# Norms whose last step ScalarE takes, with one root for a double norm, router norms by pairs, and layer 1's attentions as two lanes

## The chip, the cores and the metric

The kernel runs on one core of a Trainium2 chip. A core has engines that each work through their own instruction stream in order: TensorE (PE in the profile; its weight loads are listed as PEld), VectorE (DVE), ScalarE (ACT), GpSimd (POOL) and SyncE (SP, which only issues transfers here). They wait for each other by semaphores. Data lies in SBUF (128 partitions); TensorE's results lie in PSUM. The metric is the device time of one execution in microseconds (us); the number for a kernel is the median over runs. One further execution is profiled, and the trace tells when every instruction began and ended.

## The reference

A transformer of four layers, 4 sequences of 512 tokens, width 128, all in float32. Each layer is a "macaron": half a feed-forward part, attention, half the same feed-forward part again, each behind a layer norm without parameters.

```python
def _layernorm(x, axis=-1, eps=1e-05):
    return (x - mean(x)) / sqrt(var(x) + eps)

x = x + 0.5 * ffn_l(_layernorm(x))
x = x + attn_l(_layernorm(x))
x = x + 0.5 * ffn_l(_layernorm(x))       # l = 0, 1, 2, 3
```

The feed-forward part of layer 0 is a mixture of experts with two experts for a token, that of layer 2 one in which each expert picks its tokens, that of layer 3 one with one expert for a token. Layer 1's is dense, with ternary weights:

```python
h = silu(tlin(x, w1, s1)) * tlin(x, w2, s2)      # 128 -> 512
h = gelu(tlin(h, h1, hs1))                       # 512 -> 512
h = gelu(tlin(h, h2, hs2))                       # 512 -> 512
return tlin(h, w3, s3)                           # 512 -> 128
```

Layer 1's attention holds a layer norm of its own, with gamma and beta, so two norms follow one another there:

```python
h = _layer_norm(hidden_states, gamma, beta)
keys = h @ Wk.T + bk ; values = h @ Wv.T + bv
w = exp((keys @ Wka.T + bka) / sqrt(128))
w = w / cumsum(w, axis=1)
return cumsum(w * keys, axis=1) * values
```

The result has to be right to float32's precision, since the routers compare logits; matmuls in layer 1 split their data into three bfloat16 parts for that reason.

## The kernel before

x stays in SBUF from beginning to end as 128 partitions by 4 sequences (b) by 4 tiles of tokens (t) by 128. The program is written in one Python function. Each engine's instructions are put in order by a scheduler, which goes by what is ready and by the order in which the program issues them; the engine then keeps that order strictly, so an instruction placed too early makes all that stands behind it wait.

**Norms.** `layer_norm` (L247) does one sequence: on VectorE four `bn_stats` (L255) and four `bn_aggr` (L257) give mean and variance `mv`; `inverse_root` (L223) makes 1/sqrt(var + eps) by integer bit arithmetic and three Newton steps, 13 small instructions on 128x4 values, each needing the one before; then four `tensor_scalar` (L267), (x − mean) · root, give `xn`. With `twice` (layer 1's attention) the variance of the once normalised values is worked out (L262, L263), a second root is taken, and the two are multiplied (L265). `transposed` (L301) turns a norm on TensorE, tile `ps`, and copies it by ScalarE into xT.

**Layer 1** (`l1`, L1000 and on). The sequences go by pairs, (0, 1) and (2, 3). For each b of a pair come `first` (four groups o of six matmuls into `p`, silu on ScalarE into `sl`, the product ha_a on VectorE, L1035), and then for both b `hidden` with the first 512x512 matrix (name b) and `hidden` with the second (name c), in each four groups o of 12 matmuls with a gelu behind (L1052). `leave` (L1058 and on) multiplies by w3 (48 short matmuls into `po`) and adds to x on VectorE (L1067, L1068). `take_apart` (L990 and on) makes, after every group, the middle part `hr` on VectorE (L992) and the low part `hl` (L993), on GpSimd where o is even, on VectorE where it is odd.

The four attentions between the two feed-forward parts are generators. `pieces` is a list of such generators, and `step(pieces)` at the end of every group o runs the first of them on to its next `yield`, the next one only when that is done. So an attention's norm, its transposes (`ps_a`, after one yield), hT (L1092), the keys pk, the logits pka, the values pv, the scan cs (L1104), the reciprocal rc (L1106), two GpSimd products kw (L1107, L1108), the second scan and the product o (L1112, L1113), and the transposes back `po_a` are strewn into the matrix groups. In the same list stand the `begin`s (L1010) of the pair that comes next: norm g, transposes `ps_g`, copy, three parts. Attentions of b = 0, 1 lie in the groups of the first part's pair (2, 3); those of b = 2, 3 in the groups of the second part's pair (0, 1).

**Routers.** `l2_ffn` (loop at L1179) and `l3_ffn` (loop at L1449) go over the four b: norm (c in layer 2, d in layer 3), transposes, copy xT, four small matmuls into `lg`; `lb` (L1193 in layer 2) adds the bias to all 16 tiles of logits, and the routing begins. The loops also send x or xn to DRAM from SP. Each runs twice (0 and 1 in the names).

**Attentions of layers 2 and 3** call `layer_norm` once for each b (a2, L1384; a3, L1664). In layer 2, o_wk (L1393) and mn_k (L1375) are VectorE's steps on keys behind the projections. Layer 0 has norms of its own, in pieces, which do not use this function.

## Time and profile before

| | us |
|---|---|
| median of 3 runs (lowest, highest) | 1663.09 (1662.7, 1671.05) |
| the profiled execution | 1666.47 |
| its span, first to last instruction | 1664.7 |
| layer 0 (feed-forward, attention, feed-forward) | 0 to 562 |
| layer 1 | 562 to 855 |
| layer 2: feed-forward, attention, feed-forward | 855 to 975, to 1017, to 1135 |
| layer 3: feed-forward, attention, feed-forward | 1135 to 1271, to 1527, to 1665 |

The mean clock that TensorE was granted over the span is 0.886 of the full one. Names in the profile have their buffer numbers cut off: `xn_a` is any xn of an attention's norm, `ps_a` its transposes; of names that end in the letter of a `hidden` or `first`, `ha_a`, `hr_a` and `hl_a` are the three parts after `first`, those with b and c after the two `hidden`. A row names line, engine, operation and out<-in.

### The profile page before, as it was taken

The numbers are of one execution on the slowest core, as the hardware profiler recorded it, in microseconds if no ns is written. First come the engines' busy times: TensorE is split into PE (matmuls) and PEld (weight loads), VectorE is DVE, ScalarE is ACT, GpSimd is POOL, SyncE is SP. The second block draws the span as 40 slices with busy tenths as digits, with TensorE's granted clock in tenths as the row PEclk, the third lists the DMA queues.
The fourth block names the chain that finished last, engine by engine and source line by source line (L and its number), as shares of the span: only waits on it lengthen the run. The fifth ranks groups of instructions, "written<-read, shape, count | busy, mean of one in ns | idle before, by whom it ended". The sixth has DMA issues, their size and how long they took to land.

```text
span 1664.7 us, 24721 instructions
## 1 busy us (share of the span) xinstructions
PE 1355.9 (81%) x8372; PEld 849.3 (51%) x8372; DVE 1025.0 (62%) x3179; ACT 668.1 (40%) x1413; POOL 582.6 (35%) x811
## 2 busy tenths in 40 slices
PE   3999899999899987979983646363885899998685
PEld 2898533443698633434552534252784233334685
DVE  4547787787446678888757267625214788883311
ACT  1433477777423323333320212020342377775242
POOL 0354265450255252222210730171784110100585
PEclk9999899999899998989985867585897699998698
DMA  8022212120311010004021221023643422311445
GB/s 322 26 67 59 47 51 64 45 54 17 123 61 49 22 52 1 1 1 190 14 64 30 40 60 53 11 37 82 213 150 100 95 60 57 66 33 28 121 167 183
DMA packets 97144, 121.26 MB, mean 73 GB/s; under 512 B 12223, under 2 KB 85428, under 8 KB 95481
## 3 DMA queue, kind: packets, MB, share of 16 engines
q1 hardware_dynamic: 76393, 69.84, 14.8%
q0 software_dynamic: 15968, 44.98, 9.1%
q10 hardware_dynamic: 4656, 4.86, 0.9%
q8 instruction: 66, 1.08, 0.3%
q14 instruction: 61, 0.50, 0.1%
HBM read 91.88 MB, written 27.79 MB: 72 GB/s over the span
## 4 chain that ended last, share of the span: by engine, by line
PE 64%; DVE 14%; DMA 7%; POOL 6%; issue 5%; SPq 2%; ACT 2%; POOLq 0%; DVEq 0%; ACTq 0%
PE pa L162 9%; PE po L162 7%; PE av L162 7%; PE smax L162 6%; PE sexp L162 6%; PE pc L162 6%; PE pb L162 4%; PE p3b L162 3%; PE lg L162 2%; PE p3a L162 2%; DMA sum<-y,idx 2%; PE p L162 2%; POOL y L1608 2%; PE pq L162 1%; DVE mp L718 1%
## 5 line engine op out<-in xcount | busy, mean ns | idle before, releaser
L718 DVE TENSOR_REDUCE mp<-smax 128x1 f32<-128x512 f32 (+1 forms) x512 | 326.7, 684 | 57.3 <-PE smax L162 56.4
L756 ACT ACTIVATE e<-sexp 128x512 f32<-128x512 f32 x512 | 271.3, 599 | 99.5 <-PE sexp L162 98.4
L162 PE MATMUL smax<-keys,queries 72*128 72x512 bf16 x512 | 200.6, 403 | 11.4 <-DMA queries<-rows_q 4.6
L162 PE MATMUL sexp<-queries,keys 75*128 75x512 bf16 (+1 forms) x512 | 193.1, 388 | 6.2 <-DMA queries<-mT 4.5
L162 PEld LDWEIGHTS <-th 128*128 128x128 bf16 x768 | 74.0, 96 | 97.4 <-issue 4.8
L543 ACT ACTIVATE gl<-pa 128x256 f32<-128x256 f32 x160 | 61.3, 383 | 154.8 <-PE pa L162 115.0
L162 PEld LDWEIGHTS <-queries 72*128 72x128 bf16 x512 | 51.9, 102 | 134.3 <-issue 82.3
L1557 POOL DMA_INDIRECT xg<-xd,src x46 | 46.8, 1018 | 175.3 <-DVE wi L1547 168.1
L544 DVE TENSOR_TENSOR hid<-pa,gl 128x256 f32<-128x256 f32 x160 | 67.3, 422 | 58.7 <-ACT gl L543 58.4
L162 PE MATMUL po<-we,hid 128*128 128x128 f32 x768 | 91.7, 276 | 0.0
L162 PEld LDWEIGHTS po<-we,hid 128*128 128x128 f32 x768 | 90.7, 192 | 1.9
L610 POOL DMA_INDIRECT yg<-y,idx x64 | 66.6, 1040 | 52.5 <-DMA y<-y 42.1
L162 PE MATMUL pa<-ei,we 128*128 128x256 f32 (+1 forms) x352 | 82.7, 390 | 1.5 <-DVE x L910 0.8
L162 PE MATMUL pa<-xTe,we 128*128 128x256 f32 (+1 forms) x352 | 81.8, 381 | 1.0 <-DVE xTe L532 1.0
L162 PEld LDWEIGHTS <-keys 75*128 75x128 bf16 (+1 forms) x512 | 50.2, 100 | 57.7 <-issue 15.5
L162 PEld LDWEIGHTS pa<-ei,we 128*128 128x128 f32 (+1 forms) x352 | 67.1, 196 | 11.5 <-ACT ei L644 1.5
L361 POOL MEMSET paced<- 128x256 f32 x218 | 71.7, 329 | 0.3
L162 PE MATMUL av<-e,v 128*32 128x512 f32 x512 | 70.7, 623 | 0.0
L162 PEld LDWEIGHTS pa<-xTe,we 128*128 128x128 f32 (+1 forms) x352 | 64.6, 189 | 11.8 <-issue 1.4
L162 PE MATMUL av<-e,vp 128*32 128x512 f32 x512 | 68.7, 604 | 0.0
L496 POOL DMA_INDIRECT slots<-xn,idx x32 | 31.4, 982 | 87.7 <-DVE idx L214 82.7
L1308 POOL DMA_INDIRECT xg<-xd,idx x32 | 31.3, 977 | 86.5 <-DVE junk L1289 78.3
(446 smaller groups left out, 2934.8 us busy)
## 6 DMA issues: line engine op xcount, KB each, us to landing
we<-in_w0p_dram SPq DMA_DIRECT2D x8, 1080.0 KB
we<-in_e_pack_dram SPq DMA_DIRECT2D x8, 963.0 KB
queries<-rows SPq DMA_DIRECT2D x48, 96.0 KB
queries<-rows_q SPq DMA_DIRECT2D x48, 96.0 KB
y<-y SPq DMA_DIRECT2D x32, 128.0 KB
xd<-xn_c SPq DMA_DIRECT2D x8, 272.0 KB
slots<-zero ACTq DMA_DIRECT2D x2, 1024.0 KB
xs<-slots SPq DMA_DIRECT2D x16, 128.0 KB
```

The source lines that it names most:

```text
L162: return turn_of(nc.tensor.matmul(*a, **k))
L361: zeros = nc.gpsimd.memset(paced, 0.0)
L496: m = nc.gpsimd.indirect_dma_start(out=slots_of[half][:, :], out_offset=rows_in(idx[:, i, t : t + 1]), in_=xn[:, t, :], in_offset=None, bo ...
L543: nc.scalar.activation(gl, pa[:, 0], AF.Gelu_apprx_tanh)
L544: latest["ins"] = nc.vector.tensor_tensor(hids[e][:, c, :], pa[:, 1], gl, op=ALU.mult)
L610: m = nc.gpsimd.indirect_dma_start(out=yg[:, t, i], out_offset=None, in_=y_d[:, :], in_offset=rows_in(idx[:, i, t : t + 1]), bounds_check= ...
L718: return nc.vector.tensor_reduce(out=self.mp[i][:, t, j], in_=s, axis=AX.X, op=ALU.max, negate=True)
L756: return e, nc.scalar.activation(e, s, AF.Exp, scale=scale)
L1308: m = nc.gpsimd.indirect_dma_start(out=t, out_offset=None, in_=xd[:, :], in_offset=rows_at(e, h))
L1557: m = nc.gpsimd.indirect_dma_start(out=xg[i], out_offset=None, in_=xd[:, :], in_offset=rows_at(src, i), bounds_check=T - 1, oob_is_err=False,)
L1608: m = nc.gpsimd.indirect_dma_start(out=y_d[:, :], out_offset=rows_at(to, i), in_=y, in_offset=None, bounds_check=T - 1, oob_is_err=False,)
```

## The change

The norm's last step becomes an activation of ScalarE, Identity of rs · x + nb, with rs and nb = −mean · rs as one number for each partition; nb is one more VectorE instruction. `layer_norms` takes several sequences together and makes one root for all of them; `layer_norm` is that with one. The double norm takes one root: with var for the first norm's variance, its double root is 1/sqrt((1 + eps) · var + eps²), so only the first line of `inverse_root` differs. 144 xn instructions go from VectorE to ScalarE: 16 each of both begins g, the attentions a of layers 1, 2 and 3, and the routers c and d of both executions.

The routers go over pairs of b: one root of eight columns for a pair, both pairs of transposes, both copies, then the logits of both. xT has three buffers there, and xn in layer 3 three.

In layer 1 `pieces` keeps the begins, and the attentions stand in two lists, `attending[0]` and `attending[1]`, by b; `go_on` at each group o steps all three. Between an attention's norm and its transposes lie five yields in place of one, and one yield less in front of the second scan. `begin` has one yield more and first runs the attentions to their end. `hidden` leaves the low part to GpSimd for every o, except in the first part's pair (0, 1): 24 of the 128x512 low parts change from VectorE to GpSimd.

In the instruction streams VectorE has 2837 instructions after for 3145 before, ScalarE 1568 for 1426 (29 table loads for 31), GpSimd 840 for 816; TensorE and SP have as many as before, and SP's order is the same. In TensorE's order the transposes ps_a of b = 0 and b = 2 stood in front of the last group of `first` of the pair's first sequence, and now stand in the third group of `first` of its second sequence; those of b = 1 and b = 3 stood in the third group of that `first`, and now stand in the third group of the `hidden` that follows.

```diff
@@ -220,7 +220,7 @@
 
     behind = Behind()
 
-    def inverse_root(var, n, name, bufs=4, vector=None, eng=None):
+    def inverse_root(var, n, name, bufs=4, vector=None, eng=None, twice=False):
 
 
         def tmp(tag, dt=F32):
@@ -229,7 +229,10 @@
         vector = vector or nc.vector
         v, h, t, y = (tmp(i) for i in ("v", "h", "t", "y"))
         i = tmp("i", I32)
-        vector.tensor_scalar(v, var, EPS, None, op0=ALU.add)
+        if twice:
+            vector.tensor_scalar(v, var, 1.0 + EPS, EPS * EPS, op0=ALU.mult, op1=ALU.add)
+        else:
+            vector.tensor_scalar(v, var, EPS, None, op0=ALU.add)
         vector.tensor_scalar(i, v.bitcast(I32), 1, None, op0=ALU.logical_shift_right)
         vector.tensor_scalar(y.bitcast(I32), i, -1.0, float(0x5F3759DF), op0=ALU.mult, op1=ALU.add)
         on = eng or vector
@@ -244,31 +247,33 @@
                 on.scalar_tensor_tensor(y, t, 1.5, y, op0=ALU.add, op1=ALU.mult)
         return y
 
-    def layer_norm(pool, src, name, bufs=2, width=D, twice=False):
-
-        if not isinstance(src, list):
-            src = [src[:, t, :] for t in range(TT)]
-        st = small.tile([P, TT, 6], F32, tag="ln_st", name=f"st_{name}")
-        mv = small.tile([P, TT, 2], F32, tag="ln_mv", name=f"mv_{name}")
-        xn = pool.tile([P, TT, width], F32, tag="xn", bufs=bufs, name=f"xn_{name}")
-        for t in range(TT):
-            nc.vector.bn_stats(out=st[:, t, :], in_=src[t])
-        for t in range(TT):
-            nc.vector.bn_aggr(out=mv[:, t, :], in_=st[:, t, :])
-        rs = inverse_root(mv[:, :, 1], TT, name)
-        if twice:
-
-            v2 = small.tile([P, TT], F32, tag="ln_v2", name=f"v2_{name}")
-            nc.vector.tensor_tensor(v2, rs, rs, op=ALU.mult)
-            nc.vector.tensor_tensor(v2, v2, mv[:, :, 1], op=ALU.mult)
-            r2 = inverse_root(v2, TT, f"2{name}")
-            nc.vector.tensor_tensor(rs, rs, r2, op=ALU.mult)
-        for t in range(TT):
-            nc.vector.tensor_scalar(
-                xn[:, t, :D], src[t], mv[:, t, 0:1], rs[:, t : t + 1],
-                op0=ALU.subtract, op1=ALU.mult,
-            )
-        return xn
+    def layer_norms(pool, srcs, name, bufs=2, width=D, twice=False):
+
+        n = len(srcs) * TT
+        st = small.tile([P, n, 6], F32, tag=f"ln_st{n}", name=f"st_{name}")
+        mv = small.tile([P, n, 2], F32, tag=f"ln_mv{n}", name=f"mv_{name}")
+        nb = small.tile([P, n], F32, tag=f"ln_nb{n}", name=f"nb_{name}")
+        for i in range(n):
+            nc.vector.bn_stats(out=st[:, i, :], in_=srcs[i // TT][:, i % TT, :])
+        for i in range(n):
+            nc.vector.bn_aggr(out=mv[:, i, :], in_=st[:, i, :])
+
+
+        rs = inverse_root(mv[:, :, 1], n, name, twice=twice)
+        nc.vector.scalar_tensor_tensor(nb, mv[:, :, 0], -1.0, rs, op0=ALU.mult, op1=ALU.mult)
+        out = []
+        for q, src in enumerate(srcs):
+            xn = pool.tile([P, TT, width], F32, tag="xn", bufs=bufs, name=f"xn_{name}_{q}")
+            for t in range(TT):
+                i = q * TT + t
+                nc.scalar.activation(
+                    xn[:, t, :D], src[:, t, :], AF.Identity, scale=rs[:, i : i + 1], bias=nb[:, i : i + 1]
+                )
+            out.append(xn)
+        return out
+
+    def layer_norm(pool, src, name, **options):
+        return layer_norms(pool, [src], name, **options)[0]
 
     def norm_in_pieces(pool, src, name, bufs=1, eng=None):
 
@@ -1002,14 +1007,31 @@
 
         s1, s2, hs1, hs2 = (take(pcl, PCOL, n) for n in ("s1", "s2", "hs1", "hs2"))
         xs, act = {}, {}
-        pieces = list(aside)
+        pieces, attending = list(aside), ([], [])
 
         with tc.tile_pool(name="l1f", bufs=1, reuse_waits="tile") as wk, \
              tc.tile_pool(name="l1a", bufs=2, reuse_waits="tile") as wa:
 
+            def go_on():
+
+                step(attending[0])
+                step(attending[1])
+                step(pieces)
+
+            def finish():
+                for r in pieces + attending[0] + attending[1]:
+                    run(r)
+                for r in (pieces, *attending):
+                    r.clear()
+
             def begin(k, b):
                 nm = f"{k}_{b}"
+                for a in attending:
+
+                    while a:
+                        step(a)
                 xn = layer_norm(wk, x[:, b], f"g{nm}")
+                yield
                 yield
                 ps = tr_bank([P, S], f"ps_g{nm}")
                 for t in range(TT):
@@ -1036,7 +1058,7 @@
                         act[b].all[:, o], p2[1], s2[:, o : o + 1], sl, op0=ALU.mult, op1=ALU.mult
                     )
                     latest["ins"] = act[b].take_apart(o, nc.gpsimd if o % 2 == 0 else None)
-                    step(pieces)
+                    go_on()
 
             def hidden(k, b, w, sc, name):
                 nm = f"{k}_{b}"
@@ -1050,8 +1072,9 @@
                                 start=(c == 0 and j == 0), stop=(c == 3 and j == 2),
                             )
                     nc.scalar.activation(act[b].all[:, o], pa, AF.Gelu, scale=sc[:, o : o + 1])
-                    latest["ins"] = act[b].take_apart(o, nc.gpsimd if o % 2 == 0 else None)
-                    step(pieces)
+                    low = o % 2 == 0 or k or b > 1
+                    latest["ins"] = act[b].take_apart(o, nc.gpsimd if low else None)
+                    go_on()
 
             def leave(k, b):
                 nm = f"{k}_{b}"
@@ -1084,7 +1107,8 @@
                     return ps
 
                 xn = layer_norm(wa, x[:, b], f"a1_{b}", twice=True)
-                yield
+                for _ in range(5):
+                    yield
                 ps = tr_bank([P, S], f"ps_a1_{b}")
                 for t in range(TT):
                     transpose(ps[:, t * P : (t + 1) * P], xn[:, t, :], ident)
@@ -1106,7 +1130,6 @@
                 nc.vector.reciprocal(rc, cs)
                 nc.gpsimd.tensor_tensor(kw, kw, kT, op=ALU.mult)
                 nc.gpsimd.tensor_tensor(kw, kw, rc, op=ALU.mult)
-                yield
                 yield
                 pooled, o = tmp("pooled", 1), tmp("o")
                 nc.vector.tensor_tensor_scan(pooled, one, kw, 0.0, op0=ALU.mult, op1=ALU.add)
@@ -1127,23 +1150,19 @@
                         if last:
                             leave(*last.pop(0))
                             if k + p[0] and not (k == 1 and p[0] == 2):
-                                pieces.append(attention((b + 2) % 4))
+                                attending[b % 2].append(attention((b + 2) % 4))
                         first(k, b)
                     for b in p:
                         hidden(k, b, th1, hs1, "b")
                     if (k, p[0]) == (0, 0):
-                        for r in pieces:
-                            run(r)
-                        pieces.clear()
+                        finish()
                         then()
                     nk, nb = (k, 2) if p[0] == 0 else (k + 1, 0)
                     if nk < 2:
                         pieces += [begin(nk, nb), begin(nk, nb + 1)]
                     for b in p:
                         hidden(k, b, th2, hs2, "c")
-                    for r in pieces:
-                        run(r)
-                    pieces.clear()
+                    finish()
                     last = [(k, b) for b in p]
             for r in last:
                 leave(*r)
@@ -1176,18 +1195,18 @@
             sums_of[k, 0] = dram.tile([T, D], F32, tag=f"s{k}0", name=f"sum_{k}_0")
             xns = []
             lg = acc_bank([P, NT, NE], f"lg2_{k}")
-            for b in range(B):
-                xn = layer_norm(wk, x[:, b], f"c{k}_{b}", bufs=B, width=W)
-                xns.append(xn)
-                xT = transposed(wk, xn[:, :, :D], f"c{k}_{b}")
-                for t in range(TT):
-                    matmul(
-                        lg[:, b * TT + t, :], lhsT=xT[:, t * P : (t + 1) * P], rhs=take(mat, MAT, "wr2"),
-                        start=True, stop=True,
+            for p in ((0, 1), (2, 3)):
+                xns += layer_norms(wk, [x[:, b] for b in p], f"c{k}_{p[0]}", bufs=B, width=W)
+                xTs = [transposed(wk, xns[b][:, :, :D], f"c{k}_{b}", bufs=3) for b in p]
+                for b, xT in zip(p, xTs):
+                    for t in range(TT):
+                        matmul(
+                            lg[:, b * TT + t, :], lhsT=xT[:, t * P : (t + 1) * P], rhs=take(mat, MAT, "wr2"),
+                            start=True, stop=True,
+                        )
+                    nc.sync.dma_start(
+                        out=sums_of[k, 0][b * S : (b + 1) * S, :].rearrange("(t p) d -> p t d", p=P), in_=x[:, b]
                     )
-                nc.sync.dma_start(
-                    out=sums_of[k, 0][b * S : (b + 1) * S, :].rearrange("(t p) d -> p t d", p=P), in_=x[:, b]
-                )
             lb = tmp([P, NT, NE], "lb")
             br = take(rws, ROW, "br2").unsqueeze(1).to_broadcast([P, NT, NE])
             nc.vector.tensor_tensor(lb, lg, br, op=ALU.add)
@@ -1446,16 +1465,16 @@
             xd = dram.tile([T, D], F32, tag=f"xd{k}", name=f"xd_{k}")
             y_d = dram.tile([T, D], F32, tag=f"y3{k}", name=f"y3_{k}")
             lg = acc_bank([P, NT, NE], f"lg3_{k}")
-            for b in range(B):
-                nm = f"{k}_{b}"
-                xn = layer_norm(wk, x[:, b], f"d{nm}")
-                nc.sync.dma_start(out=xd[b * S : (b + 1) * S, :].rearrange("(t p) d -> p t d", p=P), in_=xn)
-                xT = transposed(wk, xn, f"d{nm}")
-                for t in range(TT):
-                    matmul(
-                        lg[:, b * TT + t, :], lhsT=xT[:, t * P : (t + 1) * P], rhs=take(mat, MAT, "wr3"),
-                        start=True, stop=True,
-                    )
+            for p in ((0, 1), (2, 3)):
+                xns = layer_norms(wk, [x[:, b] for b in p], f"d{k}_{p[0]}", bufs=3)
+                for b, xn in zip(p, xns):
+                    nc.sync.dma_start(out=xd[b * S : (b + 1) * S, :].rearrange("(t p) d -> p t d", p=P), in_=xn)
+                for b, xT in [(b, transposed(wk, xn, f"d{k}_{b}", bufs=3)) for b, xn in zip(p, xns)]:
+                    for t in range(TT):
+                        matmul(
+                            lg[:, b * TT + t, :], lhsT=xT[:, t * P : (t + 1) * P], rhs=take(mat, MAT, "wr3"),
+                            start=True, stop=True,
+                        )
             lb = tmp([P, NT, NE], "lb")
             br = take(rws, ROW, "br3").unsqueeze(1).to_broadcast([P, NT, NE])
             nc.vector.tensor_tensor(lb, lg, br, op=ALU.add)
```

## The prediction

> **What bounds the kernel now.** I read the page's busy shares first, then the windows of the stages that the diff touches, then who TensorE waits for in layer 1, and last the timelines of one router and of the attentions' norms.
>
> ```profile
> PE 1355.9 (81%) x8372; PEld 849.3 (51%) x8372; DVE 1025.0 (62%) x3179; ACT 668.1 (40%) x1413; POOL 582.6 (35%) x811
> ```
>
> Over the whole span TensorE is the fullest engine and ScalarE (ACT) has room; the shares are averages, so the stages decide.
>
> ```profile
> core 0: us, PE busy (x) PEld busy (x) DVE busy (x) ACT busy (x) POOL busy (x), PEclk, DMA share, GB/s
> 562.00:855.00 293.00, 263.46 (x1432) 128.02 (x1431) 237.68 (x611) 100.80 (x136) 86.95 (x89) 0.95 0.11 38
> ...
> 640.00:690.00 50.00, 41.07 (x167) 17.98 (x168) 44.82 (x126) 21.28 (x27) 12.50 (x11) 0.90 0.00 0
> 690.00:720.00 30.00, 28.73 (x207) 16.13 (x205) 24.73 (x70) 9.00 (x13) 5.76 (x6) 1.00 0.01 1
> 720.00:770.00 50.00, 39.85 (x157) 17.41 (x158) 43.43 (x125) 20.59 (x26) 11.82 (x10) 0.90 0.17 66
> ...
> 982.00:1017.00 35.00, 28.42 (x160) 21.52 (x160) 32.20 (x140) 13.14 (x21) 6.12 (x5) 0.89 0.08 24
> ```
>
> Each row is a stretch: its length, each engine's busy time, the granted clock. Layer 1 lasts 293 us and TensorE works 263 of them. Where two attentions run (640 to 690, 720 to 770), VectorE (DVE) is busy 44.8 and 43.4 of 50 us and the clock falls to 0.90, against 1.00 between. Layer 2's attention (982 to 1017) is VectorE's: 32.2 of 35.
>
> ```profile
> engine line waited for: us in total, times, longest us
> PE ps_a L165 <- DVE xn_a L267: 16.0, 2, 8.0
> PE ps_g L165 <- DVE xn_g L267: 6.4, 2, 5.5
> PE p L162 <- DVE ha_a L1035: 2.5, 2, 1.3
> ```
>
> These are TensorE's waits in layer 1 alone. Two of 8.0 us, one for each pair of attentions, are for the norm in front of the attention (637.9 and 718.7 us): its transposes were placed on TensorE before VectorE had got through the double root. The 5.5 us wait is for a norm whose x comes late from layer 0's gathers.
>
> ```profile
> 1022.45 1.11 DVE L267 TENSOR_SCALAR xn_c<-x,mv_c,ir_y_c 128x128 f32<-128x128 f32 x4
> ...
> 1024.45 1.12 DVE L267 TENSOR_SCALAR xn_c<-x,mv_c,ir_y_c 128x128 f32<-128x128 f32 x4
> ```
>
> ```profile
> 1021.56 1.88 PE L162 MATMUL lg<-mat,xT_c 128*128 128x8 f32 x8 [0.73 <-ACT xT_c L301]
> 1025.12 1.88 PE L162 MATMUL lg<-mat,xT_c 128*128 128x8 f32 x8 [0.73 <-ACT xT_c L301]
> 1028.67 1.88 PE L162 MATMUL lg<-mat,xT_c 128*128 128x8 f32 x8 [0.73 <-ACT xT_c L301]
> ```
>
> A router's end: VectorE has its last norm at 1025.6, TensorE works until 1030.5. A period of 3.55 us per b is transposes 1.09, copy of xT 0.58, lg 1.88, one after another; 0.73 of it TensorE waits for the copy.
>
> **What the new operations cost.**
>
> ```profile
> L1092 ACT ACTIVATE hT<-ps_a,pcl x4: 777/777/779, 647.1 to 739.4; 128x512 f32<-128x512 f32 x4
> ```
>
> ```profile
> L1587 ACT ACTIVATE h3a<-p3a,wd x120: 358/368/378, 1202.5 to 1647.3; 128x128 f32<-128x128 f32 x120
> ```
>
> No 128x128 Identity with scale and bias per partition stands in the trace. hT is that form at 512 columns: 0.78 us (min/median/max in ns). ScalarE's copy of that size takes 0.58, so a pointer costs about 0.10. h3a, 128x128 with one pointer, takes 0.37; one pointer more gives an estimate of 0.46 us for an xn, the value I take, as it is nearest. Bounds: 0.37 and 0.78. In a row they overlap; four h3a take 1.14 us, so with 0.09 more each I put four xn at 1.5 us and eight at 2.9. On VectorE four take 1.11.
>
> [...]
>
> **The change part by part.**
>
> VectorE loses 144 xn of 0.28 us (40 us), 24 low parts of 0.69 (16.5), and 168 short root instructions (four attentions times 16, four routers times 26), and gains 28 nb: some 75 us of 1025. ScalarE gains 144 xn, 50 to 66 us on 668. GpSimd gains 24 low parts of 1.04 (25 us). Nothing ahead of layer 1 moves.
>
> *Layer 1's start* (wait of 0.9 us at 562.5): the norm's last steps leave VectorE: 0.3 won, 0 to 0.9. The 5.5 us wait stays, since its x is late: 0.
>
> *The attentions.* In TensorE's new order the first norm's transposes of a pair stand nearly four groups of `first` later (each six matmuls of 0.222 us, 1.33), 5.3 us of work; the second norm's stand in the third group of the next `hidden`. The double root is 14 instructions shorter, which follow each other at 0.20 us: 2.8. Together 8.1, so the 8.0 us wait goes, with the 0.9 us wait for hT behind it, and the clock: 41.07 us of TensorE work at 0.90 would take about 37 at 1.00, 4.5 with the second stall's part. 13.4 us per pair are to be had. What is late next: a group of `first` needs ha 0.74, hr 0.68 and half of hl's 0.69 on VectorE, 1.8 us, against 1.33 on TensorE; with the wait no longer between, five groups in a row put TensorE 5 × 0.45 = 2.2 us ahead of ha. hT stays at 0.9. The second norm's nb stands on VectorE behind the first lane's scan (1.22), reciprocal (3.35) and second scan; its xn then go through ScalarE: 2.5. pk behind it: 1.3. Together 6.9, and I take off 1.5 for a clock that these stalls hold down. 13.4 − 6.9 − 1.5 = 5.0 per pair, two pairs 10.0. Bounds per pair: −2 (every new stall doubled) and 8. VectorE's relief of 16 xn and the roots is in these stalls already.
>
> [...]
>
> *Low parts on GpSimd.* A group of `hidden` is 12 matmuls of 0.222, 2.67 us; 1.04 on GpSimd fits, and the other b of the pair lies between maker and user. The last one is ready about 0.5 us before its use. Cost 0; without that cover 0.35 us at each of three hand-overs. What it frees on VectorE is not waited for there, so nothing is won either.
>
> *Routers by pairs.* From the last x to lb is now 13.3 us (856.9 to 870.3), 13.3 and 14.3. New: stats 0.9, aggregates 0.4, root 14 × 0.20, nb 0.2, 4.3 in all; eight xn 2.9, for both copies of xT are queued behind all eight on ScalarE; the first copy 0.6; two lg at 1.8, the second copy beside the first of them: 4.3 + 2.9 + 0.6 + 3.6 = 11.4. Won: 1.9 in each of layer 2's two, 2.9 in layer 3's second. What it costs: x of b=2 waits for the root of b=3. Layer 3's first starts from x that come one by one, so the pair's wait eats most: 0.9, between −1 and 2. Bounds for the four: 0 (xn at 0.78) and 10. The stores of x on SP keep their order and are not waited for by lg.
>
> *Layer 2's attention.* VectorE loses 16 xn, 4.4 us, in a stretch where it is full, and ScalarE (13.1 of 35) takes them between its own; o_wk and mn_k queue behind: 2.5, between 0 and 4. *Layer 3's attention:* the first xT, q and k copies now queue behind four xn on ScalarE: −0.8, between −2 and 0.
>
> Sum: 0.3 + 10.0 + 1.9 + 1.9 + 2.9 + 0.9 + 2.5 − 0.8 = 19.6 us. The profiled execution took 1666.5 us (span 1664.7), 3.4 above the median of the runs; from the median 1663.1 − 19.6 = 1643.5.
>
> **Rivals.**
>
> *A. The lanes only move the wait.* The 16 us of waits turn into the same sum at ha, o and the second norm. For it: VectorE is 90% busy there. Against: 75 us leave it. Layer 1 wins 0 to 2, the rest 9, less up to 5 where the same happens: 1653 (1651 to 1659).
>
> *B. All of it comes.* No new stall, 13.4 twice, routers and attention at their upper bounds: 27 + 9 + 4 = 40, of which I take off 8 for stages that go on into a wait for DMAs: about 1631. Against: the reciprocal and scans stay.
>
> *C. Slower: GpSimd and VectorE in each other's way.* In the trace a short root instruction that met a GpSimd low part took 1.02 us (639.2) in place of 0.16, a VectorE hl 1.65 in place of 0.69, the GpSimd one 1.5. All 24 new low parts fall in `hidden`, where lane 2's root stands between scans. If each holds VectorE 0.9 us on that chain (22 us) and ScalarE's xn wait for it with the gelu of the next group behind them, TensorE stalls in `hidden` as well. It decides once a group costs VectorE over 2.67 us; then the layer, in place of winning 10, loses 22, and the other 9 are won: 1663 + 22 − 9 = 1676. Against: hr alone is 0.68 of 2.67.
>
> [...]
>
> *D. It doesn't do what it says.* An xn on ScalarE takes 0.78 and the double root by pairs leaves x of b=2 and b=3 both late: routers 0, attentions 0, layer 1 half: about 1659.
>
> **How the numbers follow.** About 0.5% (8.3 us: below 1654.8, above 1671.4) is what a measurement here can tell from no change. Forecast 1644 (1637 to 1651): 0.50. A 0.20, half of it within 0.5%. B 0.12. C 0.10. D 0.08, within 0.5%. Faster 0.50 + 0.12 + 0.10 = 0.72; same 0.10 + 0.08 = 0.18; slower 0.10. The range is to take in B's near end, A and D: 1628 to 1664; C is left out.
>
> **What would show it.** TensorE's waits ps_a for xn at 2.5 us or less, not 8.0; layer 1 near 283 us; VectorE some 75 us less busy; xn on ScalarE at 0.46; lb about 11.4 us after the last x. Wrong if ps_a, po_a or ha waits sum to over 16 us in layer 1, if hl on GpSimd runs well over 1.04, or if layer 2's attention does not shrink.

## The result

Over 16 runs of each kernel, side by side, the changed one takes 1653.54 us (1647.96 to 1663.75) and the one before 1666.59 (1661.51 to 1675.62). The ratio is 0.9921 with a 95% interval of 0.9903 to 0.9939: 13.2 us faster, between 10.2 and 16.2. The forecast was 19.6 us. The time lies in the stated range (1628 to 1664), but above the likeliest case's own (1637 to 1651), at the figure of rival A (1653); 13.2 us off the 1663.1 that the forecast started from would be 1649.9. The profiled execution of the changed kernel took 1654.42 us (span 1652.6).

The page's busy shares of the changed kernel:

```profile
PE 1354.9 (82%) x8347; PEld 844.5 (51%) x8372; DVE 965.5 (58%) x2871; ACT 720.8 (44%) x1555; POOL 610.0 (37%) x835
```

VectorE lost 60 us of work (75 were forecast), ScalarE gained 53 and GpSimd 27, and the span lost 12: what VectorE was relieved of is mostly not what ended a stage. An xn takes 0.48 us, for 0.46 in the forecast (here those of the attentions; min/median/max in ns):

```profile
L269 ACT ACTIVATE xn_a<-x,nb_a,ir_y_a x48: 477/482/515, 639.0 to 1280.9; 128x128 f32<-128x128 f32 x48
```

TensorE's waits in layer 1, the same view as in the prediction:

```profile
PE ps_a L165 <- ACT xn_a L269: 9.6, 4, 3.6
PE ps_g L165 <- ACT xn_g L269: 5.5, 1, 5.5
PE pk L162 <- ACT hT L1116: 3.5, 4, 0.9
```

Two waits of 8.0 us have become four, 1.4 and 3.6 us in the first pair of attentions, 1.4 and 3.2 in the second. Behind the longer ones the granted clock is 0.50. TensorE's timeline at the first of them, and the windows of 2 us behind it (columns as in the prediction; the figure behind POOL's is the granted clock):

```profile
657.56 0.48 PE L165 MATMUL ps_a<-cst,xn_a 128*128 128x128 f32 x1 [3.62 <-ACT xn_a L269]
...
660.82 1.22 PE L162 MATMUL pk<-hT,mat 128*128 128x512 f32 x1 [0.87 <-ACT hT L1116]
```

```profile
657.50:659.50 2.00, 1.94 (x8) 1.69 (x9) 0.08 (x1) 1.73 (x5) 0.98 (x1) 0.50 0.00 0
659.50:661.50 2.00, 1.13 (x4) 0.56 (x3) 1.72 (x5) 0.78 (x1) 0.35 (x1) 0.50 0.00 0
661.50:663.50 2.00, 2.00 (x4) 0.45 (x3) 1.79 (x14) 0.56 (x1) 0.69 (x1) 0.50 0.00 0
663.50:665.50 2.00, 2.00 (x6) 0.74 (x5) 1.01 (x7) 0.61 (x2) 0.00 (x0) 0.50 0.00 0
665.50:667.50 2.00, 2.00 (x7) 0.82 (x6) 0.00 (x0) 0.00 (x0) 0.00 (x0) 0.62 0.00 0
667.50:669.50 2.00, 2.00 (x7) 0.79 (x6) 0.69 (x1) 1.85 (x3) 0.38 (x1) 1.00 0.00 0
```

Behind the wait, half clock lasts from 657.5 to about 667, 9.5 us, in which TensorE is busy 8.6: the 128x512 matmuls of `hidden` begin every 0.43 us there (663.55 to 666.53), for 0.22 at 1.00 (652.23 to 653.56). The clock is at half also behind the 1.4 us wait of the second pair, from 721.6 to 725.0; behind the same waits in the first pair (1.4 us for the first norm, 0.9 for hT) it stays at 1.00:

```profile
636.29:639.70 3.41, 2.01 (x10) 0.75 (x9) 3.41 (x11) 1.34 (x3) 0.00 (x0) 1.00 0.00 0
639.70:643.11 3.41, 2.45 (x9) 0.98 (x10) 3.41 (x15) 2.23 (x5) 1.04 (x1) 1.00 0.01 2
718.21:721.62 3.41, 1.62 (x7) 0.79 (x8) 3.41 (x15) 2.88 (x6) 1.04 (x1) 1.00 0.00 0
721.62:725.03 3.41, 3.41 (x7) 1.03 (x7) 3.41 (x9) 1.05 (x2) 1.40 (x1) 0.50 0.00 0
```

These windows are 3.41 us long for a reason. In the traces of both kernels all times between two changes of the clock, over the whole span, are whole multiples of 3.41 us. In the changed kernel's pairs the changes come at 656.77, 667.01, 721.62, 725.03, 738.69 and 745.51, which are 3, 16, 1, 4 and 2 times 3.41 us apart. In the 3.41 us in front of its three falls TensorE was busy 0.59, 1.62 and 0.43 us. In the first pair the grid parts the two short waits, TensorE is busy 2.01 and 2.45 us of the two stretches, and the clock stays at 1.00; in the second pair both waits fall into one, 1.62 us are busy, and the next stretch runs at half clock. So the same two waits went with either clock. The grid also lies elsewhere in each of the two executions: 641.30, a fall in the kernel before, and 656.77 here are 4.5 times 3.41 us apart.

Why the second norm is late stands in VectorE's timeline:

```profile
647.75 0.15 DVE L242 TENSOR_TENSOR ir_t_a<-ir_t_a,ir_h_a 128x4 f32<-128x4 f32 x1
647.82 1.22 DVE L1128 TENSOR_TENSOR_SCAN cs<-cst,kw 128x512 f32<-128x512 f32 x1
648.95 0.14 DVE L247 SCALAR_TENSOR_TENSOR ir_y_a<-ir_t_a,ir_y_a 128x4 f32<-128x4 f32 x1
649.07 3.35 DVE L1130 RECIPROCAL rc<-cs 128x512 f32<-128x512 f32 x1
652.34 0.10 DVE L241 TENSOR_TENSOR ir_t_a<-ir_y_a 128x4 f32<-128x4 f32 x1
...
652.95 1.24 DVE L242 TENSOR_TENSOR ir_t_a<-ir_t_a,ir_h_a 128x4 f32<-128x4 f32 x1
654.21 2.05 DVE L1135 TENSOR_TENSOR_SCAN pooled<-cst,kw 128x512 f32<-128x512 f32 x1
656.17 0.13 DVE L247 SCALAR_TENSOR_TENSOR ir_y_a<-ir_t_a,ir_y_a 128x4 f32<-128x4 f32 x1
...
656.83 0.15 DVE L263 SCALAR_TENSOR_TENSOR nb_a<-mv_a,ir_y_a 128x4 f32<-128x4 f32 x1
```

Between two steps of its root lies one long instruction of the other lane or of the ternary part. From 647.75 to the end of nb at 656.98, 9.2 us, the norm's own six short instructions (five of the root, and nb) take 1.9, and 1.24 of that is one that met a GpSimd product.

The stages of the two profiled executions, measured between the same instructions:

| stage | before | after | won | forecast |
|---|---|---|---|---|
| layer 1, first pair of attentions | 80.8 | 79.5 | 1.3 | 5.0 |
| layer 1, second pair | 82.0 | 79.4 | 2.6 | 5.0 |
| last x to lb, layer 2 (two routers) | 13.3, 14.1 | 11.2, 12.0 | 4.2 | 3.8 |
| the same, layer 3 (first, second) | 21.3, 39.9 | 19.8, 37.2 | 4.2 | 3.8 |
| layer 2's attention | 40.7 | 40.4 | 0.3 | 2.5 |
| layer 3's attention, to its first scores | 25.6 | 26.4 | −0.8 | −0.8 |

A pair runs from the first short matmul of the `leave` behind one pair of sequences to that behind the next, which is the same work in every kernel. Layer 2's second router and layer 3's two are counted from somewhat earlier events than in the prediction, the end of the attention's matmuls, the first statistics and the last scores; the differences are not touched by that. The sum is 11.8 us, and layer 1's start and rest add 0.6. What else differs between the two executions is not the change's: up to the first `hidden`, 577.1 us against 573.0, hardly anything is touched, and the twelve executions below have from 571.7 to 584.3 there; the expert stage of layer 2, 105.5 before and 108.4 after, has 105.5 to 108.9 in those twelve with the same code.

### The profile page after: what moved, and what is told of

Read it like the earlier page. It is cut to its first block, busy times and chain, and to the rows that moved or that the text cites. A ratio compares the mean times of both kernels' runs of the same rounds, so it can differ in the third digit from the quotient of the medians.

```text
span 1652.6 us, 24561 instructions
## 1 busy us (share of the span) xinstructions
PE 1354.9 (82%) x8347; PEld 844.5 (51%) x8372; DVE 965.5 (58%) x2871; ACT 720.8 (44%) x1555; POOL 610.0 (37%) x835
## 4 chain that ended last, share of the span: by engine, by line
PE 62%; DVE 14%; POOL 8%; DMA 7%; issue 5%; ACT 3%; SPq 2%; POOLq 0%; DVEq 0%; ACTq 0%
PE pa L162 9%; PE po L162 7%; PE av L162 7%; PE smax L162 7%; PE sexp L162 6%; PE pc L162 6%; PE p3b L162 3%; PE pb L162 3%; POOL y L1627 2%; DMA sum<-y,idx 2%; PE p L162 2%; PE p3a L162 2%; PE lg L162 2%; PE pq L162 1%; POOL paced L366 1%
## 5 line engine op out<-in xcount | busy, mean ns | idle before, releaser
L162 PEld LDWEIGHTS <-keys 75*128 75x128 bf16 (+1 forms) x512 | 50.2, 100 | 58.4 <-issue 14.1
L162 PEld LDWEIGHTS pa<-xTe,we 128*128 128x128 f32 (+1 forms) x352 | 64.7, 189 | 11.8 <-issue 1.4
```

What stands on the lines that cost most here:

```text
L162: return turn_of(nc.tensor.matmul(*a, **k))
```

## The experiments

Three things stood open: which part of the change won layer 1's few us, why they were few, and what ScalarE's xn and the pairs each do in the routers. Ratios are to the kernel before, run beside each kernel on the same chip (there 1687.05 us for the first four, 1667.14 for the next four, 1671.52 for the next three, and 1666.58 for the last). Since the unchanged stages scatter by some us, the length of a pair of attentions, which came out within 1.7 us, and the two together within 0.5, where the same code of layer 1 was run twice (78.3 and 81.1 with single routers, 79.5 and 79.4 in the changed kernel), says more about layer 1 than the ratio does. The third column adds up the time at half clock in each pair. It is what parts these two runs of one code: with 3.4 us less of it a pair is 1.2 us shorter, with 3.4 us more 1.7 us longer. So a difference of one such stretch between two kernels, each traced once, can be chance.

| kernel | pairs, us | half clock in them, us | longest waits in them, us | ratio, 95% interval |
|---|---|---|---|---|
| before | 80.8, 82.0 | 10.2, 10.2 | first norm 8.0 | |
| changed | 79.5, 79.4 | 10.2, 10.2 | second norm 3.6, 3.2 | 0.9921 (0.9903 to 0.9939) |
| one list again | 78.7, 79.3 | 6.8, 6.8 | first norm 5.1 | 0.9927 (0.9896 to 0.9958) |
| xn on VectorE | 80.1, 79.3 | 10.2, 6.8 | second norm 6.0 | 0.9973 (0.9948 to 0.9998) |
| routers single | 78.3, 81.1 | 6.8, 13.7 | second norm 3.6, 3.2 | 0.9909 (0.9874 to 0.9944) |
| second norm later | 78.0, 78.3 | 10.2, 6.8 | o 2.9, 3.1 | 0.9904 (0.9867 to 0.9942) |
| farther apart | 78.4, 78.4 | 6.8, 6.8 | o 3.4 | 0.9879 (0.9842 to 0.9916) |
| lanes only | 79.8, 80.9 | 10.2, 13.7 | first norm 9.4 | 0.9995 (0.9971 to 1.0019) |
| two roots | 82.7, 82.3 | 13.7, 13.7 | first norm 10.1, 9.7 | 0.9958 (0.9932 to 0.9984) |
| low parts as before | 77.3, 79.2 | 6.8, 10.2 | second norm 1.9, 3.6 | 0.9914 (0.9880 to 0.9948) |
| filled wait | 76.8, 77.6 | 3.4, 6.8 | second norm 3.6 | 0.9878 (0.9838 to 0.9919) |
| o later | 75.9, 75.5 | 6.8, 6.8 | next norm 1.7 | 0.9860 (0.9832 to 0.9888) |
| o later, low parts as before | 76.3, 75.6 | 6.8, 3.4 | next norm 2.7 | 0.9893 (0.9857 to 0.9928) |
| keys later | 75.5, 77.0 | 3.4, 6.8 | second norm 3.6 | 0.9891 (0.9872 to 0.9910) |

### One list of pieces again, the rest of the change kept

```diff
-                attending[b % 2].append(attention((b + 2) % 4))
+                pieces.append(attention((b + 2) % 4))
...
-                for _ in range(5):
-                    yield
+                yield
```

> Layer 1's attentions go back to one list of pieces (one yield between norm and transposes); ScalarE's xn, the single root, the router pairs and the low parts on GpSimd stay. Theory (the lanes move the transposes, the root only shortens the norm): the two waits for xn_a in front of the first norm come back at 5 to 6 us each instead of 8.0, the 3.6 and 3.2 us ones of the second norm go; layer 1 loses 3 to 6 us against the changed kernel: ratio to the kernel before about 0.995. Rival (the lanes bring nothing, the shorter root and VectorE's relief bring all of layer 1's gain): ratio 0.992 as the whole change.

Measured: first norm 5.1 us in both pairs, pairs 158.0 us together against 158.9 with lanes. The waits are the theory's; the time is the rival's. The lanes, placed as they are in the change, win nothing that shows on top of the rest.

### The lanes alone, and the change with two roots

```diff
-        rs = inverse_root(mv[:, :, 1], n, name, twice=twice)
+        rs = inverse_root(mv[:, :, 1], n, name)
+        if twice:
+            ...
+            r2 = inverse_root(v2, n, f"2{name}")
+            nc.vector.tensor_tensor(rs, rs, r2, op=ALU.mult)
```

The lanes alone also have xn on VectorE, single routers and the low parts of before.

> Only layer 1's lanes; xn on VectorE, two roots, routers by single sequences, low parts as before. Theory (the lanes move waits from the first norm to the second, since the norm's root shares VectorE with the first lane's scans): the pairs of attentions 79 to 83 us (80.8 and 82.0 before), a wait of 4 to 7 us in front of each second norm, ratio 0.996 to 1.000. Rival (lanes alone take away the 8.0 us waits and the clock loss, as predicted): pairs under 77 us, ratio 0.993 or less.

> The changed kernel, but with the two roots of before for layer 1's double norm. Theory (16 more short VectorE instructions at 0.2 us in each chain, the second interleaved with scans): the wait in front of each second norm grows from 3.4 to 5 to 8 us, pairs 1 to 4 us longer than the changed kernel's (79.5), ratio 0.993 to 0.997. Rival (the root is hidden by the yields): pairs the same, ratio 0.992.

Lanes alone come out at no difference. The wait that grew was not the second norm's, as I expected in both, but the first one's. TensorE's waits in the attentions' part of layer 1, with lanes alone:

```profile
PE ps_a L165 <- DVE xn_a L273: 18.7, 2, 9.4
```

Two roots in the changed kernel cost 3 us a pair, the size that the theory gave. The 9.4 is longer than the wait without lanes (8.0), although the transposes stand 5.3 us later on TensorE. VectorE's timeline of the same kernel, the second root of that norm:

```profile
638.65 0.15 DVE L264 TENSOR_TENSOR v_a<-ir_y_a 128x4 f32<-128x4 f32 x1
638.72 0.73 DVE L1062 SCALAR_TENSOR_TENSOR ha_a<-p,pcl,sl 128x512 f32<-128x512 f32 x1
639.38 0.14 DVE L265 TENSOR_TENSOR v_a<-v_a,mv_a 128x4 f32<-128x4 f32 x1
...
645.62 0.16 DVE L247 SCALAR_TENSOR_TENSOR ir_y_2a<-ir_t_2a,ir_y_2a 128x4 f32<-128x4 f32 x1
...
646.37 0.16 DVE L267 TENSOR_TENSOR ir_y_a<-ir_y_a,ir_y_2a 128x4 f32<-128x4 f32 x1
```

16 steps take 7.7 us here, since the groups of `first` that TensorE now runs in front of the transposes bring ha, hr and hl, which VectorE does between the steps. In the kernel before, where TensorE stands in its wait and brings nothing, the same 16 steps take 2.9:

```profile
642.33 0.14 DVE L262 TENSOR_TENSOR v_a<-ir_y_a 128x4 f32<-128x4 f32 x1
...
645.25 0.16 DVE L265 TENSOR_TENSOR ir_y_a<-ir_y_a,ir_y_2a 128x4 f32<-128x4 f32 x1
```

So the norm is done later by as much as TensorE has moved its use, and more. With lanes and one root the first norm's wait is 1.4 on the changed kernel and 1.6 with xn on VectorE (next), instead of 10.1 and 9.4 (the 9.4 with the low parts of before as well). Without lanes it goes from 8.0 to 5.1, near the 2.8 us that were forecast for the root; there the place of the xn and the low parts differ too, so that the root's share is not shown apart.

### xn on VectorE, and the routers by single sequences

```diff
-                nc.scalar.activation(xn[:, t, :D], src[:, t, :], AF.Identity, scale=rs[...], bias=nb[...])
+                nc.vector.tensor_scalar(xn[:, t, :D], src[:, t, :], mv[:, i, 0:1], rs[...], op0=ALU.subtract, op1=ALU.mult)
```

```diff
-            for p in ((0, 1), (2, 3)):
+            for p in ((0,), (1,), (2,), (3,)):
```

> All 144 xn go back to VectorE, the rest of the change stays. Theory (place of the xn matters little where VectorE is not what ends a stage; in layer 2's and 3's attentions the xn on ScalarE stood in front of the xT copies and took back what VectorE won): within 3 us of the changed kernel, ratio 0.990 to 0.994; first projections of layer 2's attention 9 us after its first statistics, not 9.7. Rival (relief of VectorE by 40 us is the main gain): ratio 0.997 or more.

> The routers take one sequence at a time again, xn still on ScalarE. Theory (the pairs let one root serve two and put the xT copy beside other matmuls): the times from the last x to lb go back from 11.1 to about 13 us, all four together 6 to 9 us, ratio about 0.997. Rival (the routers gained from ScalarE's xn or from a clock that came up earlier): ratio 0.992.

Both theories fell, and for one reason: the place of the xn. With pairs but xn on VectorE layer 2's routers take 13.3 and 14.1 us as before; with single sequences but xn on ScalarE 11.3 and 11.7, as after. There it is the place of the xn that wins 2 us each, not the pairs. Layer 3's first router goes the other way, 19.9 with pairs on either engine and 21.2 with single ones; its second one needs both (39.9 before, 38.6 and 38.4 with one of them, 37.2 with both). In layer 1 the second norm waits 6.0 us instead of 3.6 with xn on VectorE, of which the norm's four xn (1.11 us) may be the half. The routers' 5.6 us are most of the 8.8 by which the two ratios differ (0.9973 to 0.9921, 0.5% of 1687), and the pairs in layer 1 are 0.5 us longer. It is the rival's ratio, but the gain lies in the routers and not wherever VectorE was relieved. Layer 2's first projection came 8.9 us after the first statistics, as the theory had it, yet that attention took 40.7 us, no less than with xn on ScalarE. The ratio of the kernel with single routers does not show its loss, about 2.3 us by these stages; its interval is 12 us wide.

### Taking the waits away

The second sequence of each pair gets eight yields instead of five (theory: waits and the clock behind them are most of the pair's loss).

```diff
-                for _ in range(5):
+                for _ in range(8 if b % 2 else 5):
```

> In layer 1 the second sequence of each pair of attentions has eight yields between norm and transposes, not five, so its transposes stand two groups of hidden later; all else as in the changed kernel. Theory (the 3.6 and 3.2 us waits for the second norm cost their own length and a clock of 0.5 for some 8 us behind each): both waits under 1 us, clock 1.00 through that stretch, layer 1 shorter by 8 to 14 us, ratio 0.984 to 0.988. Rival (VectorE is what layer 1's attentions take, a wait taken away comes back at po_a, hT or the pc groups): layer 1 shorter by under 3 us, ratio 0.991 to 0.993.

The wait for the second norm went, and one of 2.9 and 3.1 us for o came, at the transposes back of the second sequence, which `begin` drains in one go; pairs 78.0 and 78.3. The rival's picture. Next seven and nine yields, with `begin` waiting for its own lane, so that nothing is drained (`finish` then runs the attentions ahead of the begins):

```diff
-                for a in attending:
-                    while a:
-                        step(a)
+                while attending[b % 2]:
+                    yield
```

> Seven yields (first sequence of a pair) and nine (second) between the attention's norm and its transposes, and begin waits for its own lane instead of running both to their end; in layers 2 and 3 the first sequence's xn is made on VectorE. Theory (layer 1's two pairs of attentions lose about 7 us each to waits of the first norm 1.4, hT 0.9, second norm 3.4, hT 0.9, o 0.5, and 3 to 4 us each to the clock behind the longest): all of these under 1 us, each pair 70 to 74 us instead of 79.5, ratio 0.980 to 0.986 to the kernel before. Rival (VectorE and GpSimd bound: the chains of scan, reciprocal and products come late wherever they are placed): pairs at 77 or more, waits at po_a and ps_g, ratio 0.990 or more.

Again a wait of 3.4 us for o, this time of the first sequence: on ScalarE its kw had come to stand behind the second sequence's four xn (1.65 us) and a table load (1.28 us), and the scans and the reciprocal start from kw. Pairs 78.4. Xn on VectorE for the first sequence in layers 2 and 3 won 1 to 1.6 us to layer 3's first scores and lost 1 to 2 in layer 2's attention. Then seven and eight yields, and one more yield in front of the first sequence's transposes back, once with the changed kernel's low parts and once with those of before:

```diff
                 nc.vector.tensor_tensor(o, pooled, vT, op=ALU.mult)
                 yield
+                if b % 2 == 0:
+                    yield
```

> As the kernel with attentions farther apart (there seven and nine yields), with seven and eight yields and one more in front of the first sequence's transposes back. Theory (the wait for o of 3.4 us was TensorE placed one group too early, and what it cost was itself and the clock behind it): no wait over 2 us in the pairs, clock 1.00 throughout, pairs 72 to 76 us, ratio 0.982 to 0.986. Rival (VectorE's and GpSimd's chain of scans and reciprocal is the bound): again a wait of 3 us in another place, pairs 78 or more, ratio 0.988.

> The same, with the low parts of odd o on VectorE as in the kernel before. [...] Rival (low parts on GpSimd bring what the change gains): pairs 2 us longer or more.

Pairs 75.9 and 75.5, ratio 0.9860 (0.9832 to 0.9888). TensorE's waits in its attentions' part:

```profile
PE ps_g L165 <- ACT xn_g L276: 3.4, 2, 1.7
PE po_a L165 <- DVE o L1141: 2.6, 2, 1.3
PE p L162 <- DVE ha_a L1062: 2.1, 2, 1.1
```

So the waits are not VectorE's chain wherever it is put: 7.5 us less in two pairs than the changed kernel, by places alone. A part of that is the clock, with 6.8 us at half in each pair instead of 10.2. The low parts of before give 76.3 and 75.6: no difference beyond 0.4 us. The clock did not stay at 1.00, though. The 1.3 us wait and the 1.7 us one follow each other within 0.6 us, and behind them:

```profile
684.00:688.00 4.00, 2.06 (x9) 1.18 (x10) 3.01 (x9) 1.98 (x5) 2.02 (x2) 0.79 0.02 4
688.00:692.00 4.00, 4.00 (x11) 1.49 (x10) 3.69 (x12) 0.82 (x2) 1.42 (x1) 0.50 0.00 0
692.00:696.00 4.00, 4.00 (x17) 1.57 (x15) 2.20 (x7) 0.69 (x1) 1.04 (x1) 0.86 0.00 0
```

### The low parts as before, and what one wait does to the clock

```diff
-                    low = o % 2 == 0 or k or b > 1
+                    low = o % 2 == 0
```

> The changed kernel, but the low parts of odd o on VectorE as before. Theory (low parts on GpSimd are hidden, but one of them stretches the second scan from 1.2 to 2.05 us while VectorE has other work less): pairs within 1.5 us of the changed kernel's, ratio 0.991 to 0.993. Rival for slower (freeing VectorE of them matters): pairs 2 to 4 us longer; rival for faster (GpSimd's contention matters): second norm's wait under 2.5 us, pairs 2 us shorter or more.

Pairs 77.3 and 79.2, together 2.4 us less than the changed kernel's: the low parts on GpSimd bring nothing to these pairs that shows. That they cost anything is not shown either, as the first pair has 6.8 us at half clock for 10.2 in the changed kernel. The scan that one of them stretches takes 2.04 us here too, so neither rival holds, though the first pair has the numbers of the second one (a wait under 2.5 us, 2.2 us less). The second norm waits 1.86 us in one pair and 3.61 in the other, one code twice in one execution. In the first pair the clock had already been at half, from 642.4 to 649.2, behind waits of 1.41 us for the first norm and 0.91 for hT; TensorE came later to the transposes, and so waited less. In the second pair the same two waits (1.35 and 0.91) left it at 1.00. TensorE's two waits for the second norm and a window behind each:

```profile
659.80 0.33 PE L165 MATMUL ps_a<-cst,xn_a 128*128 128x128 f32 x1 [1.86 <-ACT xn_a L269]
...
735.75 0.47 PE L165 MATMUL ps_a<-cst,xn_a 128*128 128x128 f32 x1 [3.61 <-ACT xn_a L269]
```

```profile
660.00:663.00 3.00, 2.09 (x11) 1.20 (x10) 2.38 (x7) 2.14 (x5) 0.59 (x1) 1.00 0.00 0
```

```profile
738.50:741.50 3.00, 2.48 (x4) 0.94 (x5) 2.83 (x17) 0.78 (x2) 1.04 (x1) 0.50 0.00 0
```

The clock is 1.00 behind the shorter wait here and 0.50 behind the longer one.

### Useless work in the wait, and the keys a group later

```diff
                 ps = tr_bank([P, S], f"ps_a1_{b}")
+                for _ in range(10 if b % 2 else 0):
+                    matmul(ps, lhsT=bfc[:, :P], rhs=th1[:, 0, :], start=True, stop=True)
```

> The changed kernel with ten useless matmuls of 0.22 us each in front of the transposes of each second norm, so that TensorE idles about 1.4 us there instead of 3.6; what the wait is for comes no earlier. Theory (a wait of 3.2 us or more takes the clock to half for some 7 us behind it, a shorter one does not): granted clock 1.00 behind the wait, the pairs of attentions 2 to 4 us shorter each in spite of the added work, 75.5 to 77.5. Rival (the clock there falls for another reason, or the stall itself is the whole loss): pairs at 79 to 80 as in the changed kernel, clock 0.5 to 0.6 behind the wait.

The wait was not filled. Of the useless matmuls six ran beside the first norm's transposes and four one group ahead of the wait; counted from the pair's start TensorE came to the wait, and xn came, 0.5 us earlier in the first pair than in the changed kernel, and TensorE idles 3.6 us as before. Yet the pairs are 76.8 and 77.6. Nor had the changed kernel's clock stayed at 1.00 behind every wait under 3.2 us: behind the 1.4 us one of its second pair it was 0.50 for 3.4 us. What went were the 0.9 us waits for hT: the first norm's, where the useless matmuls stand, and the one behind the long wait, as matmuls of `hidden` had come to stand in between. The half clock behind the long wait lasted 3.5 and 5.4 us instead of 9.5 and 7.3. So the last kernel takes away only the wait for hT behind the long one:

```diff
                 nc.scalar.activation(hT, ps, AF.Identity, ...)
                 yield
+                if b % 2:
+                    yield
```

> The changed kernel with one more yield between hT and the keys of the second sequence of each pair, so that a full group of hidden stands between its transposes and pk. Theory (after the 3.6 us wait the clock comes back some 3 us later if TensorE is kept busy, and the 0.9 us wait for hT right behind puts that off to 7 to 8 us): the 3 us wait stays, the wait for hT goes, the clock is back 3 to 5 us behind the wait, pairs 2 to 3 us shorter, 76.5 to 77.5. Rival (the clock stays down some 7 us after any such wait): pairs 0.9 us shorter, 78.5 to 79.

TensorE's wait in the first pair and the windows behind:

```profile
656.73 0.47 PE L165 MATMUL ps_a<-cst,xn_a 128*128 128x128 f32 x1 [3.61 <-ACT xn_a L269]
```

```profile
656.10:658.10 2.00, 1.37 (x5) 0.76 (x6) 0.65 (x2) 1.91 (x5) 1.49 (x1) 0.56 0.00 0
658.10:660.10 2.00, 2.00 (x8) 1.05 (x7) 0.69 (x1) 0.82 (x2) 0.89 (x1) 0.58 0.00 0
660.10:662.10 2.00, 2.00 (x13) 1.17 (x11) 0.00 (x0) 0.62 (x2) 0.15 (x1) 1.00 0.00 0
```

The same wait of 3.6 us, the clock back after 3.1 us instead of 9.5, the pair at 75.5 instead of 79.5: 4.0 us, of which the waits that went (hT 0.9, o 0.45) are 1.3 and the clock is the rest. In the second pair half clock lasted from 731.4 to 738.3, 6.8 us, two stretches of the grid as behind the changed kernel's 3.2 us wait, and the pair took 77.0. What that pair won besides the waits is the stretch that the changed kernel spent at half clock behind the first norm, from 721.6, which this edit does not touch. The first 3.41 us at half clock differ in the two pairs. In the first the clock fell 0.4 us before the wait ended, TensorE was busy 89% of them, and the clock came back; in the second it fell 0.7 us before, TensorE was busy 79%, and one more stretch ran at half. So the theory holds in the first pair. In the second its time came, but not for its reason, and how much of the 4.0 us another execution would show is open.

## Why the prediction was right in its sign and high in its size

*Layer 1's attentions* (10.0 us forecast, 3.9 measured) are the step that failed, and in it the term of the clock. For each pair 2.0 us less waiting were forecast (8.9 gone, 6.9 new) and 3.0 us from the clock (4.5 won, 1.5 taken off). The two pairs before, and then the two after (TensorE's busy time stands first):

```profile
628.25:709.04 80.79, 69.79 (x373) 34.11 (x372) 70.34 (x194) 30.28 (x40) 19.00 (x17) 0.94 0.00 1
709.04:791.09 82.05, 70.63 (x374) 34.44 (x373) 70.39 (x194) 30.27 (x40) 19.01 (x17) 0.94 0.25 97
623.62:703.10 79.48, 71.76 (x366) 34.67 (x372) 61.59 (x143) 35.18 (x55) 27.90 (x24) 0.94 0.00 1
703.10:782.55 79.45, 72.19 (x366) 34.60 (x373) 61.03 (x142) 35.20 (x55) 28.94 (x25) 0.94 0.25 100
```

TensorE stands 3.3 and 4.2 us less, more than forecast, as the old waits for ha, silu and o, 2.1 and 2.6 us a pair, shrank to 0.45. But the same matmuls (the traces lack a few records of them) take 2.0 and 1.6 us longer: the clock cost time where it was to give 3.0. That has two causes. The 4.5 were worked out from 41.07 us of work at a mean clock of 0.90, but this mean also counts time in which TensorE stood. Behind the old waits it worked only 4.7 and 5.9 us at half clock (645.9 to 651.5 and 726.7 to 733.5), so that at most 2.4 and 3.0 us were to be had. And the new waits brought back 10.2 us of half clock in each pair, 8.6 and 9.4 of them at work, where 1.5 us had been taken off, an estimate for which no trace or run gives a figure.

The new waits themselves came near enough one by one: 1.4 instead of 2.2 at the end of `first`, hT 0.9, the second norm 3.6 and 3.2 instead of 2.5, hT 0.9 instead of pk's 1.3, o 0.45. That the first of them is so short is luck, though. "Together 8.1, so the 8.0 us wait goes" put the norm's end at a fixed time, from which 5.3 us of later use and 2.8 of shorter root (15 instructions less by the diff, not 14) could be taken. The lanes alone show that the norm's end moves with what TensorE is given to do in front of it: 9.4 us of wait in place of 8.0. With lanes the one root was worth 7.8 to 8.7 us at that place; the lanes' own part was nothing.

Short waits went with half clock as well: behind waits of 1.4 and 0.9 us (the changed kernel's second pair) it was 0.50 for 3.4 us, though TensorE had worked for 1.62 of the 3.41 us in front, and behind waits of 1.3 and 1.7 us (o later) for 6.8 us.

*Routers* (7.6 forecast, 8.4 measured): the sum was right and its reason half wrong. In layer 2 the pairs were credited with what ScalarE's xn won alone.

*Layer 2's attention* (2.5 forecast, 0.3 measured): VectorE's relief was real, 34.9 us of work for 38.0 in the stage, but what lies behind the first projection became only 1.1 us shorter (31.8 to 30.7). And the first xT copy stood on ScalarE behind six xn, so that the first projection began 9.7 us after the first statistics instead of 8.9. That is the term that was set at −0.8 for layer 3's attention and was left out here. That −0.8 came out there to the digit is luck: the changed kernel's code has 25.6 to 26.7 us in that stage in these runs, against 25.6 before.

*Low parts on GpSimd* at 0: within 0.4 us a pair in the two kernels without waits over 2.7 us that differ in them alone, and 2.4 us against them, over both pairs, in the changed kernel, which had one stretch more at half clock. *xn at 0.46*: 0.48.

*The rivals.* A, lanes that only move the wait, gave the better time, 10 us for the 13.2 measured against the forecast's 19.6, but not for its reason: the waits of the two pairs became 7.4 us shorter, and the clock took 3.5 of that back. C did not come: VectorE's scan took 2.05 us while GpSimd made a low part, for 1.23 alone, and 2.04 with the low parts of before as well; what that stretching costs the pairs was not measured.

## What to carry to other kernels

A norm whose root is a chain of short dependent steps does not end at a fixed time: on an engine that is kept in order every step may stand behind one long instruction of other work, and then shortening the chain can be worth more than its own length (here 7.8 to 8.7 us of wait for 16 steps that take 2.9 in the kernel before), while using its result later may be worth nothing (a wait of 9.4 us instead of 8.0 with lanes alone). After moving waits, compare the granted clock behind them, not only their sum: here two pairs with the same wait of 3.6 us differ by 4.0 us, and only 1.3 of that is other waits. As one code took 78.3 and 81.1 us in the two pairs of one trace, with 6.8 and 13.7 us at half clock, a difference of a few us between two single traces has to be checked against the time at half clock. If a wait can't be avoided, put a full group of matmuls behind it before the next thing that may wait: with the keys a group later the clock came back 3.1 us behind the 3.6 us wait instead of 9.5, in one pair of the two.

## What the runs showed of the hardware that was not expected

In the traces of both kernels the granted clock changed only on a grid of 3.41 us, whose place differs between the two executions (641.30 and 656.77). In the pairs of the fourteen traces it was at half for 3.4, 6.8, 10.2 or 13.7 us, and for no other length. In the pairs of those two traces it fell five times; in the 3.41 us in front of a fall TensorE was busy 0.05 and 0.00 us in the kernel before, and 0.59, 1.62 and 0.43 in the changed one, where it stayed at 1.00 behind 2.01 us (636.29 to 639.70). All five times it came back behind a stretch in which TensorE was busy all of the 3.41 us, and it stayed at half behind one with 2.77 (660.18 to 663.59); with the keys later it came back behind 89% and stayed at half behind 79%. Two waits of 1.3 and 1.7 us, 0.6 us apart, were followed by 6.8 us at half, while waits of 1.4 and 0.9 us were in some pairs and not in others.

A step of 0.16 us on VectorE took 1.02 us (kernel before, 639.21), and a scan 2.05 instead of 1.23 (changed kernel, 654.21), while GpSimd worked on a 128x512 tensor_tensor, which itself took 1.51 instead of 1.04 beside the step and 1.03 beside the scan. A step with one input tile, a tensor_scalar of 0.17, took 1.02 as well (kernel before, 614.81), while an ha of 128x512 that lay wholly beside such a tensor_tensor took 0.75 (570.90), as it does alone.
